# W ahead of the adjacency rows, the short row tile in the middle of its sums, and gathers of names and rows by turns, in a four-layer graph and expert network

## The chip, the cores and the metric

The kernel runs on one core of one Trainium2 chip, as one launch. The metric is the time of that launch on the device in microseconds (us), the median of several runs; less is better. The core's engines are TensorE (PE in the profile; its weight loads are PEld), VectorE (DVE), ScalarE (ACT), GpSimd (POOL) and SyncE (SP). In this kernel SP issues the large loads, and POOL issues the small loads and all indirect DMAs, the gathers and scatters by index.

## The reference

`x` is 2708 x 256, `adj` is 2708 x 2708, all float32. There are four layers, each of a graph step that adds a product with a matrix made from `adj`, and an expert or dense step. The change touches layers 0 and 1. `layernorm` is over the last axis. Cut to these two:

```python
# layer 0, graph step
msg = layernorm(x) @ W + B
weights = where(adj < 1.0, exp(-(1 / adj - 1) ** 2 / (2 * 0.5 * 0.5)), 0)
x = x + weights @ msg
# layer 0, experts: the best two of eight, softmax of their two scores
...
# layer 1, graph step
A = adj + eye(2708)
D = 1 / sqrt(sum(A, axis=1))
x = x + relu((A * D[:, None] * D[None, :]) @ (layernorm(x) @ W) + b)
# layer 1, experts: one hidden layer for all, then the best of eight second matrices
xf = layernorm(x)
H = gelu(xf @ W1 + b1)                 # 2708 x 1024
probs = softmax(H @ Wg + bg)
out = zeros_like(xf)
for e in range(8):
    y = H @ Wd[e] + bd[e]
    out = out + where(argmax(probs) == e, probs[:, e] * y, 0)
x = x + out
```

Layers 2 and 3 are two attention layers over the same neighbours, one with two experts for all rows and one with a dense step.

## The kernel before

**Tiles.** The 2708 rows make 22 row tiles of 128; the last one, number `FULL` = 21, has 20 rows (`LAST`). A graph step is done for a group of output tiles at a time, which hold their sums in PSUM: layer 0 has groups of 9, 7 and 6 tiles (`GROUPS`), layer 1 of 8, 8 and 6 (`GROUPS1`). For each group the loop over `j` goes over the row tiles of `adj`: a piece `adrow` of 128 rows and the group's columns is loaded by SP, made into weights, and multiplied into the group's sums. In layer 0 the weights need ACT and DVE (`y`, `wt`, L813 to L824), in layer 1 only the diagonal is added (L1096), and a mask of the positive entries is kept for the later layers (L1093). In layer 0 these products are at L863, in layer 1 at L1124.

**The last row tile.** Its 20 rows would use 20 of TensorE's 128 rows. `last_rows` (L278) fills a tile with ones by a memset on POOL and loads the 20 rows into its four quadrants with several small DMAs on SP (L282); `last_product` (L286) then multiplies from these quadrants. In layer 0 this happens inside the loop, in layer 1 it is the last pass of the loop, `j == FULL`, and its products end the sums (`stop`).

**The start.** Layer 0 begins with the products of `layernorm(x) @ W` as the first group's loop goes along: `W` is loaded by POOL through `mat` (L127), its column sums come from four matmuls (L796), DVE subtracts them (L798), and L241 multiplies a tile of transposed `x` with the result. `xT` and `x` are loaded by SP, two tiles at a time, between the rows of `adj` (L806, L56, L838).

**Layer 1's experts.** After each group, `send1` computes the hidden rows (L347 and on), writes them to the DRAM tensor `hid` (L1047), finds each row's expert, and scatters the row's number and score into `taken` at places sorted by expert (`route`, then L481). A unit of the expert step is 128 places of one expert, and class `Units` handles it: a gather of the 128 row numbers and scores (`fetch_names`, L495), a gather of those hidden rows, 512 KB, into one of three buffers (`fetch_rows`, L625), the expert's second matrix, 1152 KB, by SP into one of three buffers `wb` (`weights1`, L971), the transposition of the rows (L635, copied by ACT at L636), 16 matmuls (L674), bias and score on DVE (L675, L676), and a scatter to `given` (L481). Nine units (`NA`) can be known from the first two groups; `begin` prepares them within the third group's sums, and the first of them are run between the steps of the third group's `send1`. The other 15 wait for its scatters. `more` (L646) issues names and rows so that at most four units have names fetched and three have rows.

**Order.** The program's order on each engine is that of a scheduler, within the data dependences; `pin()` fixes what came before it, and manual edges with no wait (`NoSync`) can fix the order of two instructions on their engine. All indirect DMAs go through POOL one after the other; a DMA on POOL also waits for the one issued eight before it, and one on SP for an earlier one of its lane in the same way. The buffers `wb` lie where the sums' buffers were, so W2's first reads wait for the end of the third group's sums. The layers' small vectors and matrices come on POOL as well; layer 3's `w_l3` (L1210) is loaded there while layer 1's units run, and `score_columns` (L250, L251) multiplies it on DVE.

Of the kernel before, what the change touches and what calls it, by code (L numbers as in the profile page):

```python
# [8 lines left out]
F32 = mybir.dt.float32  # L9
# [6 lines left out]
P = 128  # L16
N = 2708
D = 256
DC = D // P
E = 8  # L20
NT = (N + P - 1) // P
W = 512
Q = P // 4

FULL, LAST = N // P, N % P
# [41 lines left out]
def adj_ffn4(ctx: ExitStack, tc: tile.TileContext, a: dict, out: bass.AP):  # L67
    nc = tc.nc
# [75 lines left out]

    pin()

    def rsqrt(pool, val, n):


        y = pool.tile([P, n], F32, name="rs_y", tag=f"rs_y{n}", bufs=2)  # L150
        q = pool.tile([P, n], F32, name="rs_q", tag=f"rs_q{n}", bufs=2)
        v.tensor_scalar(q.bitcast(I32), val.bitcast(I32), 1, None, op0=ALU.logical_shift_right)
        v.tensor_scalar(y.bitcast(I32), q.bitcast(I32), -1.0, float(0x5F3759DF), op0=ALU.mult,
                        op1=ALU.add)
        for _ in range(3):
            v.tensor_tensor(q, y, y, ALU.mult)
            v.scalar_tensor_tensor(q, q, -0.5, val, op0=ALU.mult, op1=ALU.mult)
            v.scalar_tensor_tensor(y, q, 1.5, y, op0=ALU.add, op1=ALU.mult)
        return y
# [115 lines left out]
                      stop=True, tile_position=(0, z))  # L275
        s.copy(values, p[:, :n])

    def last_rows(dst, parts):  # L278

        g.memset(dst, 1.0)  # L280
        for q, k, c0, w in parts:
            nc.sync.dma_start(dst[q * Q : q * Q + LAST, k : k + w],  # L282
                              a["adjT"][FULL * P :, c0 : c0 + w])
# [209 lines left out]
    def gather(dst, src, ix, bound, group, past):  # L493

        i = g.indirect_dma_start(out=dst, out_offset=None, in_=src,  # L495
                                 in_offset=bass.IndirectOffsetOnAxis(ap=ix, axis=0),
                                 bounds_check=bound, oob_is_err=False)
        tc.declare_no_dep(i.ins, group=group, keep=past, reason="rows of other groups")
        tc.add_to_no_dep_group(group + "read", i.ins)
        behind(i, past)  # L500


    XW = D + 2
# [96 lines left out]
    class Units(Blocks):  # L600
# [2 lines left out]

        def __init__(self, pool, given, weights, hidden):
            Blocks.__init__(self, pool, given, weights)
            self.hidden, self.named, self.places = hidden, [], [0, 0]

            self.names = pool.tile([P, MOST, 2], F32, name="names")
            g.memset(self.names, 1.0)
            self.hs = pool.tile([P, 3, HC * P], F32, name="hs")  # L610
            g.memset(self.hs, 0.0)
            self.ik, self.ok = "taken1", "given1"

        def fetch_names(self, item):
            (_, ix, _), b, past, src, full = item
            m = self.names[:, self.places[0], :]
            self.places[0] += 1
            gather(m, src, ix[:, b, :], src.shape[0] - 1, self.ik, past)
            self.named.append((m, src.shape[0]))

        def fetch_rows(self):
            m, n = self.named.pop(0)
            h = self.hs[:, self.places[1] % 3, :]
            self.places[1] += 1
            g.indirect_dma_start(out=h, out_offset=None, in_=self.hidden[:n, :],  # L625
                                 in_offset=bass.IndirectOffsetOnAxis(ap=m[:, 0:1].bitcast(I32), axis=0),
                                 bounds_check=n - 1, oob_is_err=False)
            self.rows.append((m, h))

        def turn(self, pool, h):  # L630
# [92 lines left out]
    with ExitStack() as l0:  # L723
# [17 lines left out]
        gate, gnn, sums = ExitStack(), ExitStack(), ExitStack()  # L741
        tp = gate.enter_context(tc.tile_pool(name="t0", reuse_waits="tile", bufs=2))
        gp = gnn.enter_context(tc.tile_pool(name="g0", reuse_waits="tile", bufs=3))
        w_sb = mat(gp, "L0_gnn_W", D)
        b_bc = row_bc(gp, "L0_gnn_B", D)
        wg = mat(tp, "L0_ffn_Wg", E)
        bg = row_bc(tp, "L0_ffn_bg", E)
# [78 lines left out]
        for tiles in GROUPS:  # L826
# [8 lines left out]
            for j in range(FULL):  # L835
                r = rows(j)
                ad = gp.tile([P, GMAX * P], F32, name="adrow", bufs=5)[:r, :w]
                i = nc.sync.dma_start(ad, a["adjT"][j * P : j * P + r, c0 : c0 + w])  # L838
                reads.append(i.ins.name)
                if begin and j % 2 == 0:  # L840
                    for t0 in (j,) if j < FULL - 3 else (j, j + 2) if j == FULL - 3 else ():
                        front(t0)
                if begin and j == FULL - 2:
                    spread_out(msg[:, FULL, :])
                if j == (FULL - 2 if begin else 12):
                    cols = [gp.tile([P, GMAX * P], F32, name=name, tag=name, bufs=bufs)[
                        :, : (1 + max(k for _, k in places.values())) * P]
                            for name, bufs in (("adrow", 5), ("y", 3), ("wt", 4))]
                    last_rows(cols[0], [(places[n][0], places[n][1] * P, c0 + n * P,
                                         min(2, len(own) - n) * P) for n in range(0, len(own), 2)])  # L850
                    weigh(*cols, P)
                    for n, t, _ in by_turns(own):
                        last_product(acc[n // 2][:, n % 2, :], places[n][0], cols[2],
                                     places[n][1] * P, msg[:, FULL, :], False)
                y = gp.tile([P, GMAX * P], F32, name="y", bufs=3)[:r, :w]
                wt = gp.tile([P, GMAX * P], F32, name="wt", bufs=4)[:r, :w]
                weigh(ad, y, wt, r)
                for p, pair in zip(acc, pairs):
                    for n in pair:
                        if n == len(own):  # L860
                            continue
                        _, k, q = own[n]
                        te.matmul(p[:q, n - pair[0], :], lhsT=wt[:, k : k + q],  # L863
                                  rhs=msg[:r, j, :], start=(j == 0 and n == pair[0]),
                                  stop=(j == FULL - 1 and n == pair[-1]))
                if end and j == 2:
                    cols = [gp.tile([P, GMAX * P], F32, name=name, tag=name, bufs=bufs)[
                        :, : NT * Q].rearrange("p (t c) -> p t c", c=Q)
                            for name, bufs in (("adrow", 5), ("y", 3), ("wt", 4))]
                    last_columns(cols[0])  # L870
                    weigh(*cols, P)
                    last = last_sums(acc[-1].rearrange("p k d -> p (k d)"), cols[2],
                                     lambda j, r: msg[:r, j, :], D)
                    v.tensor_tensor(x[:LAST, FULL, :], x[:LAST, FULL, :], last, ALU.add)
                if end and j == NT - 5:
                    past = list(scattered["taken0"])
                    items = [(full, b, past, taken[0][: 2 * held], True) for b in range(NA)]
                    for item in items[:2]:
                        work0.fetch_rows(item)
# [81 lines left out]
    with ExitStack() as l1:  # L961
# [2 lines left out]
        b1 = tp.tile([P, HC], F32, name="b1")  # L964
        g.dma_start(b1, a["L1_ffn_b1"])
        hw = l1.enter_context(tc.tile_pool(name="h1", side="right", reuse_waits="tile", bufs=1))
        wbs = {}

        def weights1(b, e):
            wb = wbs["pool"].tile([P, 2048 + D], F32, name="wb", bufs=3)  # L970
            nc.sync.dma_start(wb, a["L1_ffn_Wdp"][bass.ds(e, 1)].rearrange("e p n -> p (e n)"))  # L971
            return wb.rearrange("p (f d) -> p f d", d=D)

        gate, gnn, sums = ExitStack(), ExitStack(), ExitStack()
# [91 lines left out]
        for tiles in GROUPS1:  # L1066
# [11 lines left out]
                v.scalar_tensor_tensor(x[:q, t : t + m, :], o, 0.0, x[:q, t : t + m, :],  # L1078
                                       op0=ALU.max, op1=ALU.add)

            for j in range(NT):
                r = rows(j)
                if j == FULL:

# [2 lines left out]
                        spread_out(sup[:, FULL, :])  # L1087
                ad = gp.tile([P, 8 * P], F32, name="adrow", tag="adrow", bufs=4)[:r, :w]
                if j < FULL:
                    nc.sync.dma_start(ad, a["adjT"][j * P : j * P + r, c0 : c0 + w])  # L1090
                else:
                    last_rows(ad, [(q, 0, c0, w) for q in range(P // Q)])
                v.tensor_scalar(mask[:r, j, c0 : c0 + w], ad, 0.0, None, op0=ALU.is_gt)  # L1093
                for t, k, q in own:
                    if t == j:
# [18 lines left out]
                if j == FULL:  # L1114
                    for n, t, k in by_turns(own):
                        last_product(acc[n // 2][:, n % 2, :], n // 2, ad, k, sup[:, FULL, :],
                                     n == pairs[n // 2][-1])
                    continue
                for p, pair in zip(acc, pairs):
                    for n in pair:  # L1120
                        if n == len(own):
                            continue
                        _, k, q = own[n]
                        te.matmul(p[:q, n - pair[0], :], lhsT=ad[:, k : k + q],  # L1124
                                  rhs=sup[:r, j, :], start=(j == 0 and n == pair[0]), stop=False)
            for p, pair in zip(acc, pairs):
                if pair[0] < len(own):
                    t, m = own[pair[0]][0], len(pair)
# [602 lines left out]
```

## Time and profile before

| | |
|---|---|
| median of 3 runs | 2036.22 us (2031.78 to 2037.07) |
| the profiled execution, its span | 2048.93 us, 2047.2 us |
| mean granted TensorE clock | 0.967 of full speed |
| TensorE, from the page | 1916.4 us busy in 9641 instructions |
| DMA | 243.93 MB, mean 119 GB/s over the span |

The profiled execution is one run, recorded with its instructions; its times in the views are us from the start of its span. The whole span in 40 equal slices of 51 us, each digit a busy share in tenths (PEclk: the granted clock, GB/s: what the DMA engines moved):

```profile
PE   7999979999997999999796889999999999999997
DVE  7687842543434333344341165555445588987876
ACT  8777722222224203022221152223234400120112
POOL 1004362333321000102345300000000000000000
PEclk9999979999998999999897999999899999999998
DMA  8435567877744343534666720000101000000000
```

Layer 0's graph step fills slices 1 to 5, and its experts those up to about 632 us. Layer 1's sums run from there to 996 us, its third group from 881; the units and the third group's `send1` from 996 to 1168 (slices 20 to 23). Layers 2 and 3 follow. The queues that the change moves work between or reorders, with packets, MB and share of the 16 DMA engines' time (q1 is SP's, q0 is POOL's):

```profile
q1 hardware_dynamic: 69596, 196.81, 29.0%
q0 software_dynamic: 17232, 45.38, 6.5%
```

In the groups of waits, a line names the engine and the line that waited, what it waited for, and then the total in us, how many times, and the longest one. In the timeline, a line is start, length, engine, line, operation, output and inputs, count, and in brackets how long the engine had been idle before it and what ended that. By line a helper's number can stand for several tiles, so the tile's name is read with it.

### The profile page before, as it was taken

Reading aid. Unit: us, or ns where it says so; the run is one execution under the profiler, and the core shown is the slowest. Engines: PE = TensorE matmul, PEld = TensorE weight load, DVE = VectorE, ACT = ScalarE, POOL = GpSimd, SP = SyncE. Lnnn points to the kernel's source line nnn. Section 1 sums busy time; section 2 is a strip of 40 time slices with the busy share of each in tenths; the row PEclk is TensorE's granted clock in tenths of the full one; section 3 lists DMA queues with packets and bytes.
Section 4 is the critical chain, followed back from the end, with each engine's and each line's share of the span. In section 5 each row is a group of like instructions: output and inputs, shape, how many; then the busy total and the mean of one; then the engine's idle time right before and its main releaser. Section 6 shows DMA issues by size and latency. Waiting matters only on the chain.

```text
span 2047.2 us, 25961 instructions
## 1 busy us (share of the span) xinstructions
PE 1916.4 (94%) x9641; PEld 1374.6 (67%) x9641; DVE 1103.8 (54%) x2503; ACT 639.0 (31%) x1407; POOL 333.0 (16%) x369
## 2 busy tenths in 40 slices
PE   7999979999997999999796889999999999999997
PEld 5888868888886788878675768887576522232334
DVE  7687842543434333344341165555445588987876
ACT  8777722222224203022221152223234400120112
POOL 1004362333321000102345300000000000000000
PEclk9999979999998999999897999999899999999998
DMA  8435567877744343534666720000101000000000
GB/s 267 144 101 156 171 219 269 324 289 303 268 175 126 119 137 111 144 86 121 200 200 234 304 69 1 1 1 1 41 1 32 16 1 21 21 26 11 16 11 24
DMA packets 86960, 243.93 MB, mean 119 GB/s; under 512 B 17151, under 2 KB 40919, under 8 KB 77612
## 3 DMA queue, kind: packets, MB, share of 16 engines
q1 hardware_dynamic: 69596, 196.81, 29.0%
q0 software_dynamic: 17232, 45.38, 6.5%
q8 instruction: 79, 1.29, 0.3%
q14 instruction: 53, 0.43, 0.1%
HBM read 216.54 MB, written 28.97 MB: 120 GB/s over the span
## 4 chain that ended last, share of the span: by engine, by line
PE 55%; issue 5%; DMA 5%; DVE 4%; POOL 3%; ACT 2%; POOLq 0%; SPq 0%; DVEq 0%; ACTq 0%
PE num L1643 11%; PE ps_acc L1319 9%; PE acc L1124 8%; PE ps_tmp L347 7%; PE den L1654 6%; PE ps_acc L1495 3%; PE ps_tmp L241 3%; DMA given<-ys,xs 2%; PE ps_tmp L198 1%; PE ps_acc L241 1%; PE ps_tmp L1045 1%; POOL given L481 1%; POOL names L495 1%; PE yacc L674 1%; DMA adrow<-in_adjT 1%
## 5 line engine op out<-in xcount | busy, mean ns | idle before, releaser
L1638 DVE SCALAR_TENSOR_TENSOR e<-arena,G,mask 128x1024 f32<-128x1024 f32 (+2 forms) x264 | 294.2, 1150 | 41.1 <-PE den L1654 40.7
L1643 PE MATMUL num<-e,wh 128*64 128x512 f32 (+4 forms) x1056 | 240.9, 553 | 0.3 <-ACT L_gnn_W L1176 0.3
L1124 PE MATMUL acc<-sup,adrow 128*128 128x256 f32 x882 | 200.7, 385 | 2.8 <-DVE o L1076 1.5
L1319 PE MATMUL ps_acc<-hh,e 128*128 128x257 f32 x882 | 199.2, 382 | 2.0 <-ACT o L1264 2.0
L863 PE MATMUL acc<-msg,wt 128*128 128x256 f32 x882 | 198.1, 381 | 2.4 <-DVE x L886 1.2
L1124 PEld LDWEIGHTS acc<-sup,adrow 128*128 128x128 f32 x882 | 166.4, 192 | 31.0 <-issue 4.6
L578 PE MATMUL ps_acc<-xTs,wa 128*128 128x256 f32 x768 | 179.5, 387 | 6.1 <-issue 3.3
L863 PEld LDWEIGHTS acc<-msg,wt 128*128 128x128 f32 x882 | 165.2, 190 | 28.1 <-DVE wt L824 2.1
L1319 PEld LDWEIGHTS ps_acc<-hh,e 128*128 128x128 f32 x882 | 163.7, 190 | 29.6 <-ACT o L1264 5.0
L1643 PEld LDWEIGHTS num<-e,wh 128*64 128x64 f32 (+1 forms) x1056 | 73.9, 136 | 153.2 <-issue 119.9
L587 PE MATMUL yacc<-wb,hTs 128*128 128x256 f32 x768 | 175.5, 381 | 0.5 <-DVE ys L589 0.5
L580 ACT ACTIVATE hTs<-ps_acc,wa 128x256 f32<-128x256 f32 x192 | 90.8, 475 | 259.4 <-PE yacc L587 172.0
L578 PEld LDWEIGHTS ps_acc<-xTs,wa 128*128 128x128 f32 x768 | 142.1, 192 | 35.2 <-ACT hTs L580 5.3
L587 PEld LDWEIGHTS yacc<-wb,hTs 128*128 128x128 f32 x768 | 145.2, 191 | 20.3 <-DVE ys L589 0.9
L1654 PE MATMUL den<-e,wh 128*32 128x512 f32 (+4 forms) x1056 | 138.2, 553 | 0.0
L1313 DVE SCALAR_TENSOR_TENSOR e<-Rb,G,mask 128x640 f32<-128x640 f32 (+2 forms) x110 | 85.2, 775 | 92.8 <-PE ps_acc L1319 92.7
L199 ACT COPY xT<-ps_tmp 128x256 f32<-128x256 f32 x120 | 40.7, 364 | 276.5 <-PE ps_tmp L198 275.4
L1093 DVE TENSOR_SCALAR mask<-adrow 128x1024 uint8<-128x1024 f32 (+1 forms) x66 | 41.4, 630 | 134.5 <-DMA adrow<-in_adjT 134.5
L674 PE MATMUL yacc<-wb,hTs 128*128 128x256 f32 x384 | 94.7, 400 | 7.6 <-DVE ys L675 3.8
L589 DVE TENSOR_TENSOR ys<-yacc,wb 128x256 f32<-128x256 f32 x48 | 20.4, 424 | 134.3 <-PE yacc L587 134.3
L1654 PEld LDWEIGHTS den<-e,wh 128*32 128x32 f32 (+1 forms) x1056 | 30.9, 108 | 90.0 <-issue 86.7
L674 PEld LDWEIGHTS yacc<-wb,hTs 128*128 128x128 f32 x384 | 75.1, 202 | 19.2 <-DVE ys L675 4.1
(423 smaller groups left out, 2660.4 us busy)
## 6 DMA issues: line engine op xcount, KB each, us to landing
adhalf<-in_adjT SPq DMA_DIRECT2D x42, 677.0 KB
wb<-in_L_ffn_W2p SPq DMA_DIRECT2D x24, 1152.0 KB
wb<-in_L_ffn_Wdp SPq DMA_DIRECT2D x24, 1152.0 KB
wa<-in_L_ffn_W1b SPq DMA_DIRECT2D x24, 1028.0 KB
adrow<-in_adjT SPq DMA_DIRECT2D x42, 512.0 KB
adrow<-in_adjT SPq DMA_DIRECT2D x42, 320.0 KB
adrow<-in_adjT SPq DMA_DIRECT2D x21, 576.0 KB
hid<-hrow POOLq DMA_DIRECT2D x21, 512.0 KB
```

The source lines that it names most:

```text
L347: te.matmul(p[:, :w], lhsT=w1[:, c, f * P : (f + 1) * P], rhs=xnT[:, c, c0 : c0 + w], start=(c == 0), stop=(c == DC - 1))
L578: te.matmul(p[:, f % 2, :], lhsT=w1[:, c, f * P : (f + 1) * P], rhs=xT[:, c, :], start=(c == 0), stop=(c == DC - 1))
L580: s.activation(hT[:, f, :], p[:, f % 2, :], AF.Gelu, bias=bias[:, f : f + 1])
L587: te.matmul(q[:, k, :], lhsT=hT[:, f, k * P : (k + 1) * P], rhs=w2[:, f, :], start=(f == 0), stop=(f == HC - 1))
L674: te.matmul(q, lhsT=hT[:, f, :], rhs=w2[:, f, :], start=(f == 0), stop=(f == HC - 1))
L863: te.matmul(p[:q, n - pair[0], :], lhsT=wt[:, k : k + q], rhs=msg[:r, j, :], start=(j == 0 and n == pair[0]), stop=(j == FULL - 1 and n == ...
L1124: te.matmul(p[:q, n - pair[0], :], lhsT=ad[:, k : k + q], rhs=sup[:r, j, :], start=(j == 0 and n == pair[0]), stop=False)
L1313: v.scalar_tensor_tensor(e[:r, :w], Rb[:r, c0 : c0 + w], G[:r, j, :], mask[:r, j, c0 : c0 + w], op0=ALU.max, op1=ALU.mult)
L1319: te.matmul(p[:, : D + 1], lhsT=e[:, k : k + q], rhs=hh[:, j, :], start=(j == 0), stop=False)
L1638: v.scalar_tensor_tensor(e[:r, :w], Rb[:r, k, :w], G[:r, j, 2 * pair + k, :], mask[:r, j, c0 : c0 + w], op0=ALU.max, op1=ALU.mult)
L1643: te.matmul(num[k * DK : (k + 1) * DK, hf, :q], lhsT=wh[:r, j, 2 * pair + k, :DK], rhs=e[:r, h0 - c0 : h0 - c0 + q], start=(j == 0), stop= ...
L1654: te.matmul(den[z : z + Q, :q], lhsT=wh[:ri, i, 2 * pair + k, DK : DK + 1].to_broadcast([ri, Q]), rhs=e[:ri, h0 - c0 : h0 - c0 + q], start ...
```

## The change

Four edits in layers 0 and 1. No arithmetic is added or left out.

- Layer 0's `W` is loaded by SP, as its first read, and each read of `adj` is kept behind the one before it, the first behind `W`.
- In layer 1 the short row tile `FULL` is taken after row tile 11 and not after 20, in every group; row 20 now ends the sums. The fill with ones is done there by DVE (`v`) and not by POOL; in layer 0 it stays on POOL (`g`).
- Each read of `wb` in layer 1 is kept behind the last read of `adj` that the program issued before it.
- In `Units`, each gather of names is kept behind the last gather of rows that the program issued before it (`self.got`). `gather` returns its instruction for this.

`after` adds an edge of order with no wait.

```diff
+    def after(i, past):
+
+        tc.add_manual_dep(i.ins, past, mybir.DependencyInfo(
+            mybir.DependencyClass.NoSync, mybir.DependencyReason.DATA), reason="order")
...
-    def last_rows(dst, parts):
-
-        g.memset(dst, 1.0)
+    def last_rows(dst, parts, filler):
+
+        filler.memset(dst, 1.0)
...
         behind(i, past)
+        return i
...
-            self.hidden, self.named, self.places = hidden, [], [0, 0]
+            self.hidden, self.named, self.places, self.got = hidden, [], [0, 0], None
...
-            gather(m, src, ix[:, b, :], src.shape[0] - 1, self.ik, past)
+            i = gather(m, src, ix[:, b, :], src.shape[0] - 1, self.ik, past)
+            if self.got is not None:
+
+                after(i, self.got)
...
-            g.indirect_dma_start(out=h, out_offset=None, in_=self.hidden[:n, :],
+            i = g.indirect_dma_start(out=h, out_offset=None, in_=self.hidden[:n, :],
...
+            self.got = i.ins.name
...
-        w_sb = mat(gp, "L0_gnn_W", D)
+        w_sb = gp.tile([P, DC, D], F32, name="L0_gnn_W", bufs=1)
+        first = nc.sync.dma_start(w_sb, a["L0_gnn_W"].rearrange("(c p) n -> p c n", p=P))
...
                 i = nc.sync.dma_start(ad, a["adjT"][j * P : j * P + r, c0 : c0 + w])
+                after(i, reads[-1] if reads else first.ins.name)
                 reads.append(i.ins.name)
...
-        wbs = {}
+        wbs, reads = {}, []
...
-            nc.sync.dma_start(wb, a["L1_ffn_Wdp"][bass.ds(e, 1)].rearrange("e p n -> p (e n)"))
+            i = nc.sync.dma_start(wb, a["L1_ffn_Wdp"][bass.ds(e, 1)].rearrange("e p n -> p (e n)"))
+            after(i, reads[-1])
...
-            for j in range(NT):
+            for j in [*range(12), FULL, *range(12, FULL)]:
...
-                    nc.sync.dma_start(ad, a["adjT"][j * P : j * P + r, c0 : c0 + w])
+                    i = nc.sync.dma_start(ad, a["adjT"][j * P : j * P + r, c0 : c0 + w])
+                    reads.append(i.ins.name)
                 else:
-                    last_rows(ad, [(q, 0, c0, w) for q in range(P // Q)])
+                    last_rows(ad, [(q, 0, c0, w) for q in range(P // Q)], v)
...
-                                     n == pairs[n // 2][-1])
+                                     False)
...
-                                  rhs=sup[:r, j, :], start=(j == 0 and n == pair[0]), stop=False)
+                                  rhs=sup[:r, j, :], start=(j == 0 and n == pair[0]),
+                                  stop=(j == FULL - 1 and n == pair[-1]))
```

More of the change, by code (lines that the diff above doesn't have):

```diff
@@ L849, in adj_ffn4 @@
                     last_rows(cols[0], [(places[n][0], places[n][1] * P, c0 + n * P,
-                                         min(2, len(own) - n) * P) for n in range(0, len(own), 2)])
+                                         min(2, len(own) - n) * P) for n in range(0, len(own), 2)], g)
                     weigh(*cols, P)
```

## The prediction, written before the change was run

> **What bounds the kernel now.** I read the page's busy shares and chain first, then TensorE's own waits, then the busy time by stage, last the timeline where those waits lie.
>
> ```profile
> PE 1916.4 (94%) x9641; PEld 1374.6 (67%) x9641; DVE 1103.8 (54%) x2503; ACT 639.0 (31%) x1407; POOL 333.0 (16%) x369
> ...
> PE 55%; issue 5%; DMA 5%; DVE 4%; POOL 3%; ACT 2%; POOLq 0%; SPq 0%; DVEq 0%; ACTq 0%
> ```
>
> TensorE is busy 94% of the span, so a change that leaves its work alone can win only its waits and the stretches at a lower granted clock. The waits that the change can reach:
>
> ```profile
> PE ps_tmp L796 <- DMA L_gnn_W<-in_L_gnn_W: 9.2, 1, 9.2
> PE acc L286 <- DMA adrow<-in_adjT: 7.8, 1, 7.8
> PE ps_acc L635 <- DMA hs<-hid,names: 7.3, 2, 6.6
> PE ps_tmp L241 <- DVE L_gnn_W L798: 6.0, 1, 6.0
> PE ps_acc L635 <- ACT hTs L636: 5.1, 2, 3.2
> PE yacc L674 <- DVE ys L675: 3.8, 1, 3.8
> ```
>
> By stage (columns: length; busy us and count of PE, PEld, DVE, ACT, POOL; granted clock; DMA share; GB/s):
>
> ```profile
> 20.00:40.00 20.00, 20.00 (x89) 17.33 (x88) 18.45 (x36) 18.28 (x21) 0.00 (x0) 1.00 0.84 277
> 986.00:1007.00 21.00, 11.04 (x44) 8.63 (x45) 11.33 (x39) 2.95 (x6) 7.25 (x8) 0.67 0.65 214
> 1047.00:1116.00 69.00, 48.62 (x233) 41.01 (x233) 17.02 (x60) 9.77 (x18) 45.60 (x47) 0.85 0.71 220
> 1116.00:1160.00 44.00, 43.26 (x239) 38.28 (x238) 7.78 (x20) 10.74 (x20) 18.30 (x18) 1.00 1.00 399
> ```
>
> From 20 us on layer 0's sums fill TensorE, so time won ahead of them stays won. At 986 and from 1047 to 1116 TensorE has holes and a low clock; in the second POOL is busy 45.6 of 69 us with 47 instructions. From 1116 TensorE is full again, beside DMA at 1.00. The two holes:
>
> ```profile
> 989.89 1.00 POOL L495 DMA_INDIRECT names<-taken,b_ix  x1 [0.30 <-issue]
> 990.89 0.65 POOL L280 MEMSET adrow<- 128x640 f32 x1
> 991.56 1.42 SPq L282 DMA_DIRECT2D adrow<-in_adjT  x4
> 993.47 2.45 PE L286 MATMUL acc<-sup,adrow 20*128 20x256 f32 x10 [7.81 <-DMA adrow<-in_adjT]
> 995.84 3.17 PE L635 MATMUL ps_acc<-ident,hs 128*128 128x128 f32 x16
> 1001.31 4.08 PE L674 MATMUL yacc<-wb,hTs 128*128 128x256 f32 x10 [2.29 <-DMA wb<-in_L_ffn_Wdp]
> ```
>
> The sums are over at 985.65. The filler memset of the last row tile stands behind four gathers of names on POOL, the tile's loads behind the memset, and TensorE idles 7.81 us.
>
> ```profile
> 1072.27 0.99 POOL L625 DMA_INDIRECT hs<-hid,names  x1 [0.30 <-issue]
> 1078.80 1.03 POOL L625 DMA_INDIRECT hs<-hid,names  x1 [0.30 <-issue]
> 1080.55 1.94 PE L635 MATMUL ps_acc<-ident,hs 128*128 128x128 f32 x8 [6.57 <-DMA hs<-hid,names]
> 1097.94 0.77 POOL L1210 DMA_DIRECT2D w_l<-in_L_gnn_WT  x1
> 1110.23 2.22 PE L674 MATMUL yacc<-wb,hTs 128*128 128x256 f32 x6 [3.83 <-DVE ys L675]
> ```
>
> An indirect DMA holds POOL 1.0 us and 0.3 us more; three or four names between two gathers of rows put 6.5 to 8.5 us between rows, where a unit (16 matmuls L674, 3.47, and 8 of L635, 0.87) needs 4.33. The layer-3 matrix, last in POOL's queue, lands 9.8 us later (1107.74); DVE has waited 9.57 us for it at L250, ahead of the sum `ys`, and TensorE waits for DVE.
>
> **What the Trainium skill says.** "DMA: Bandwidth & Descriptors", Anatomy of one DMA: a POOL-issued DMA costs about 2.0 us plus bytes over 436 GB/s, and waits sit on the issuing sequencer, not in the DMA engines. Where the DMA engines are quiet (1090), names land 2.0 to 2.4 us after issue, which agrees; the 256 KB W takes 7.1, because (same page, Issuing engines are not separate DMA queues) all queues share 16 engines: its neighbours are six reads of SP's. "TensorE: Matmul & The Clock Gate", Part 1: an idle window of about 3.4 us halves the clock; the 0.67 at 986 agrees. "VectorE: DVE Perf Modes", Zero memsets can be issued as uint32: a memset takes a cycle per element whatever the type, so I scale below.
>
> **Part 1, layer 0.** W now goes first on SP; POOL loses one issue. All of SP's reads move one issue (0.4 us) and 256 KB back, about 0.8 us at the 313 GB/s of 0 to 20 us. W was issued at 1.91 and landed at 9.03; issued at 0.83 with nothing ahead it lands at about 5 (adrow 0 did, at 4.97). The pair of L798, which DVE ran at 16.74 behind statistics and weights, stands ahead of them in the new order. TensorE then can start L241 when xT of tile 2 is there (it landed at 14.6, plus 0.8: 15.4); three tiles of L241 stand before row 0. Before, row 0's sums began at 21.63; now at about 16 to 18. Row 1's weights come at 21.9 at best, since ACT has one layer-norm waiting for adrow 3 (about 18.5) ahead of them. So by 21.9 one row (18 records, 3.97) and one tile of L241 (0.93) more are done: 4.9, taken as 5. Bounds: 1 (row 0 itself waits for ACT) to 8 (row 1 isn't late either).
>
> **Part 2, layer 1's last row tile.** FULL goes between rows 11 and 12 in three groups; its memset moves from POOL (1.51 or 0.65 us) to DVE: 128x128 took 0.17 us, so 1024 columns some 1.1 to 1.4 us by the page's rule. DVE is busy 18.7 of 39 us in the last group, which hides it; in the middle group it stands ahead of one diagonal sum that TensorE needs: up to 1.5 us, 0.5 taken. Its four SP loads are tiny, but in the last group they fall among the taken scatters, where reads land 5.7 to 7.6 us after issue; TensorE idled 0.96 there at 966.6 and may idle 3. So the sums end at 985.65 plus 10 matmuls at full clock (16 took 1.15, so 0.7) plus 2 more idle, less 0.8 where it overlaps: 987.5, against 995.92: 8.4. Behind it work runs at a higher clock: L635 x16 at 2.1 and not 3.17, L674 x10 at 2.3 and not 4.08. W2's reads still can't start before the sums' buffers are free (0.1 us after their end; landing 5.1 later), so the idle of 2.29 stays. 8.4 + 2.8 less 0.5 = 10.7; bounds 5 (idle of 7 in the middle) to 13. Order edges of W2's reads behind adj's only fix what the queue does now: nothing.
>
> **Part 3, names and rows by turns.** The number of indirect DMAs is the same. In POOL's new order a unit is given, rows, names: 3 x 1.31 = 3.93, under 4.33. By hand, with the route some 10 us earlier (about 1037), the six scatters issued 1040 to 1048 and landed near 1053, first names 1055, rows of unit 10 at 1060.6, landed 1066.5. DVE now waits for the layer-3 matrix before the seventh `ys` (issued about 1058.6, landed by 1068), so the weights' slot for unit 10 frees late: its L674 at 1075, with about 6 + 4 us of idle around it. Before, it started at 1087.31; units 10, 11, 12 then took 28.3 us to 1115.6 instead of 13.0. So 12.3 + 15.3 = 27.6 ahead, of which 10.7 is part 2's: 16.9. Against it: (a) the short halts at 1091 to 1098 (3 x 1.13 "issue", 3.17 for ACT), which have no cause on POOL: half of 6.6 kept, 3.3; (b) names now stand in the saturated stretch. Rows k+2 need names issued five instructions earlier, 2c - 1.31 us, c the time of a unit. Names follow a rows gather in the same queue, and rows landed +9.5 there, so names would land at +8.4, asking c = 4.85. But fewer rows would be in flight then, and names are small (their packets take 0.01 us): I take 4.4, between 4.33 and 4.85: 15 x 0.07 = 1. Part 3: 12.6; bounds 3 and 18.
>
> **Sum.** 5 + 10.7 + 12.6 = 28.3. The profiled execution took 2048.93 (span 2047.2), so about 2020.6; it stands 12.7 above the median 2036.22 of the runs shown, which gives 2007.9. I forecast 2008. Layers 2 and 3 (1180 to 2047) aren't touched.
>
> **Rivals.**
> A, the units give it back: names late in the queue (c = 4.85 costs 15 x 0.52 = 7.8), all halts stay (3.3 more). For it: DMA is at 1.00 from 1116, so no earlier start shortens that. Against: the window 1047 to 1116 moves only 220 GB/s. Gain 28.3 - 10.1 = 18: 2018.
> B, layer 0's start isn't kept: ACT (18.28 of 20) and DVE (18.45) are nearly as full as TensorE at 20 to 40, and row 1 onward may pace by them. Gain 23: 2013, inside the forecast's range.
> C, slower: the turn serialises. Rows wait on POOL for names, and everything behind (given, next names) waits with them. It loses when 15(c - 4.33) exceeds 28.3 + 1, c = 6.3, which needs names to land 2c - 1.31 = 11.3 us after issue; at c = 6.9 it is 10 slower: 2046. For it: taken scatters at +10.0, rows at +9.8. Against: names never over 7.1.
> D, it doesn't do what it says: W shares the engines with adrow and lands as late, the last row's idle just moves, c is near 5: 2034.
>
> **How the numbers follow.** About 0.3% (6 us) is what a measurement can tell from no change. Forecast (2001 to 2016, B in it) 0.56; A (2016 to 2026) 0.23; below 2001 0.04; D 0.07; C 0.10. Faster 0.83, same 0.07, slower 0.10. The range 1999 to 2029 leaves out C and most of D.
>
> **What would show it.** Step 1: first L863 before 18. Step 2: no wait at L286 over 4, sums over before 989. Step 3: rows at most 5.5 us apart on POOL, unit 10 before 1078, units at 4.3 to 4.5. It is wrong if TensorE waits for `hs` in every unit, or if the DVE stall on the layer-3 matrix reaches TensorE for more than 6.

## The result and the profile after

| | before | after |
|---|---|---|
| median, us (4 runs each) | 2036.64 (2031.78 to 2040.77) | 2012.41 (2009.97 to 2015.35) |
| profiled execution, its span, us | 2048.93, 2047.2 | 2009.97, 2008.2 |

The ratio is 0.9883, with a 95% interval of 0.9857 to 0.9908: 24 us less, between 19 and 29. The forecast was 2008, which is 28 us less.

The two profiles are 39 us apart, more than the medians. Layer 0's experts, which nothing in the change touches, took 349.8 us from first to last matmul at L578 (L584 after) in the profile of before and 342.9 in that of after. The experiments below show that this belongs to the session and not to the kernel. So from here on stages are compared, within one session where there is a pair.

The page's line of TensorE and the waits of TensorE in the profile after (columns: who waited for whom; us in total, times, longest). Lines have moved: L246 was L241, L291 was L286, L645 was L635, L684 was L674, L807 was L796.

```profile
PE 1902.1 (95%) x9641; PEld 1364.3 (68%) x9641; DVE 1106.0 (55%) x2506; ACT 636.7 (32%) x1407; POOL 329.5 (16%) x365
```

```profile
PE ps_acc L645 <- DMA hs<-hid,names: 10.9, 7, 5.4
...
PE ps_tmp L246 <- DMA xT<-in_xT: 6.2, 1, 6.2
...
PE yacc L684 <- DMA wb<-in_L_ffn_Wdp: 3.9, 4, 2.6
PE ps_tmp L807 <- DMA L_gnn_W<-in_L_gnn_W: 3.9, 1, 3.9
...
PE acc L291 <- DMA adrow<-in_adjT: 2.8, 1, 2.8
```

Every wait of the prediction's list has got shorter or gone, but one: the wait for `W` is 3.9 and not 9.2, VectorE's step on it (L798, 6.0) is at 0.5, the one at the last row tile 2.8 and not 7.8, those for `ys` and for `hTs` don't appear. The wait for rows has grown from 7.3 in two places to 10.9 in seven. At the start the wait for `W` has a successor, 6.2 us for `xT`.

The start of layer 0 on TensorE (timeline):

```profile
3.86 2.05 PE L807 MATMUL ps_tmp<-L_gnn_W,all_ones 128*128 128x256 f32 x4 [3.86 <-DMA L_gnn_W<-in_L_gnn_W]
6.42 3.78 PE L246 MATMUL ps_tmp<-L_gnn_W,xT 128*128 128x256 f32 x8 [0.52 <-DVE L_gnn_W L809]
16.42 3.78 PE L246 MATMUL ps_tmp<-L_gnn_W,xT 128*128 128x256 f32 x8 [6.22 <-DMA xT<-in_xT]
19.99 4.29 PE L875 MATMUL acc<-msg,wt 128*128 128x256 f32 x18
```

`W` is there 5.3 us sooner, but the sums start only 1.6 sooner (19.99 against 21.63): behind the first two tiles of `x`, two more stand ahead of row 0 in TensorE's order. Their `xT` comes at 16.4, and their 8 matmuls run at a granted clock of 0.50 (16 to 20 us).

The end of layer 1's third group (timeline):

```profile
951.24 1.66 PE L291 MATMUL acc<-sup,adrow 20*128 20x256 f32 x10 [2.84 <-DMA adrow<-in_adjT]
952.83 21.37 PE L1138 MATMUL acc<-sup,adrow 128*128 128x256 f32 x90
974.04 2.91 PE L645 MATMUL ps_acc<-ident,hs 128*128 128x128 f32 x24
979.58 5.38 PE L684 MATMUL yacc<-wb,hTs 128*128 128x256 f32 x16 [2.63 <-DMA wb<-in_L_ffn_Wdp]
```

The last row tile stands in the middle, with 2.84 us of idle. Behind the sums the wait for the first W2 is still there, and the 16 matmuls after it take 5.38 us, where 16 of them at full clock take 3.62: the granted clock over them is 0.68.

The stages (columns: length; busy us and count of PE, PEld, DVE, ACT, POOL; granted clock; DMA share; GB/s), the second one from unit 10 on:

```profile
1026.00:1062.00 36.00, 29.03 (x154) 25.20 (x155) 13.69 (x53) 6.05 (x12) 26.35 (x29) 0.91 0.83 264
1062.00:1106.00 44.00, 40.21 (x217) 34.33 (x216) 7.60 (x20) 9.39 (x18) 27.44 (x28) 1.00 0.95 351
```

Before, the full stretch of units had TensorE busy 43.26 of 44 us beside DMA at 1.00. Now this stretch begins 88 us after the sums and not 120, but has TensorE at 40.21 and DMA at 0.95: something else holds it. POOL's timeline shows what:

```profile
1077.26 1.00 POOL L500 DMA_INDIRECT names<-taken,b_ix  x1 [0.31 <-issue]
1078.56 1.02 POOL L486 DMA_INDIRECT given<-ys,names  x1 [0.30 <-issue]
1079.89 1.02 POOL L634 DMA_INDIRECT hs<-hid,names  x1 [0.30 <-PE yacc L684]
1081.22 1.00 POOL L500 DMA_INDIRECT names<-taken,b_ix  x1 [0.31 <-issue]
1083.45 1.01 POOL L486 DMA_INDIRECT given<-ys,names  x1 [1.23 <-DVE ys L686]
1086.82 1.01 POOL L634 DMA_INDIRECT hs<-hid,names  x1 [2.36 <-PE ps_acc L645]
```

The gather of rows at 1086.82 uses the names issued five instructions earlier, at 1077.26. The profile puts its 2.36 us down to a TensorE turn, but the buffer's own turn (of the rows issued three gathers earlier) had been over since 1080.5. By the trace's semaphore updates those names landed at 1086.08, 8.8 us after their issue and 0.74 before the rows' start. The same for the last gathers in a row:

```
rows issued   their names issued   landed            from landing to issue
1086.82       1077.26              1086.08 (+8.8)    0.74
1090.76       1081.22              1089.97 (+8.8)    0.79
1095.82       1088.14              1095.07 (+6.9)    0.75
1101.40       1092.09              1100.66 (+8.6)    0.74
1105.76       1097.14              1105.02 (+7.9)    0.74
1110.18       1102.73              1109.44 (+6.7)    0.74
```

The names in turn landed 0.2 to 0.7 us after the 512 KB of rows that had been issued just before them (for the six: 1085.91, 1089.24, 1094.90, 1100.07, 1104.84 and 1109.09). So here the names set the pace. From unit 10 to the last, a unit takes 4.78 us (1061.62 to 1128.61, 14 steps); in 11 of these 15 units the rows start within 1 us of their names' landing, in the other four 2.3 to 4.7 us after it.

### The profile page after: what moved, and what is told of

Its sections match the earlier page's. It is cut to its first block, busy times and chain, and to the rows that moved or that the text cites. A ratio compares the mean times of both kernels' runs of the same rounds, so it can differ in the third digit from the quotient of the medians.

```text
span 2008.2 us, 25964 instructions
## 1 busy us (share of the span) xinstructions
PE 1902.1 (95%) x9641; PEld 1364.3 (68%) x9641; DVE 1106.0 (55%) x2506; ACT 636.7 (32%) x1407; POOL 329.5 (16%) x365
## 5 line engine op out<-in xcount | busy, mean ns | idle before, releaser
L584 PE MATMUL ps_acc<-xTs,wa 128*128 128x256 f32 x768 | 177.1, 384 | 2.0 <-DVE xTs L557 1.9
L593 PE MATMUL yacc<-wb,hTs 128*128 128x256 f32 x768 | 174.1, 379 | 0.5 <-DVE ys L595 0.5
L584 PEld LDWEIGHTS ps_acc<-xTs,wa 128*128 128x128 f32 x768 | 141.2, 191 | 30.4 <-DVE xTs L557 5.3
L593 PEld LDWEIGHTS yacc<-wb,hTs 128*128 128x128 f32 x768 | 144.1, 190 | 19.6 <-DVE ys L595 1.1
L684 PE MATMUL yacc<-wb,hTs 128*128 128x256 f32 x384 | 91.8, 390 | 3.9 <-DMA wb<-in_L_ffn_Wdp 3.9
L835 DVE SCALAR_TENSOR_TENSOR wt<-adrow,wt 128x640 f32<-128x640 f32 (+3 forms) x67 | 71.0, 1061 | 27.2 <-ACT wt L141 26.6
```

What stands on the lines that cost most here:

```text
L584: te.matmul(p[:, f % 2, :], lhsT=w1[:, c, f * P : (f + 1) * P], rhs=xT[:, c, :], start=(c == 0), stop=(c == DC - 1))
L593: te.matmul(q[:, k, :], lhsT=hT[:, f, k * P : (k + 1) * P], rhs=w2[:, f, :], start=(f == 0), stop=(f == HC - 1))
L684: te.matmul(q, lhsT=hT[:, f, :], rhs=w2[:, f, :], start=(f == 0), stop=(f == HC - 1))
```

## The experiments

Each kernel was timed in turns with before on the same chip. There were three sessions, each on another chip, on which before's own median was 2048.15, 2038.88 and 2048.05 us; so across sessions the ratios are the safer comparison. "us" is the ratio's difference from 1 times before's 2036.64. The stages come from one profile of each: layer 1's sums (start of the first matmul to start of the last), and the rest (from there to the start of the last unit's last matmul).

| kernel | ratio, 95% interval | us | layer 1's sums | the rest |
|---|---|---|---|---|
| session 1: before again | - | - | 322.2 | 172.2 |
| W first | 0.9982 (0.9968 to 0.9996) | -3.7 | 322.8 | 174.4 |
| row in the middle | 0.9945 (0.9924 to 0.9966) | -11.2 | 312.1 | 166.8 |
| turns | 0.9936 (0.9916 to 0.9957) | -13.0 | 318.7 | 162.0 |
| session 2: the whole change | 0.9877 (0.9857 to 0.9898) | -25.1 | 311.5 | 158.8 |
| five names ahead | 0.9893 (0.9871 to 0.9916) | -21.8 | 311.7 | 155.5 |
| layer 3's matrix late | 0.9906 (0.9888 to 0.9923) | -19.1 | 310.4 | 168.6 |
| fill on VectorE alone | 0.9970 (0.9957 to 0.9982) | -6.1 | 315.7 | 177.1 |
| session 3: middle, fill on POOL | 1.0009 (0.9994 to 1.0024) | +1.8 | 327.7 | 166.9 |
| without the turns | 0.9909 (0.9880 to 0.9937) | -18.5 | 310.2 | 167.8 |
| five ahead for the rest | 0.9862 (0.9837 to 0.9887) | -28.1 | 311.0 | 158.9 |

**The parts one by one.** Before plus the edits of one part:

```diff
# W first
-        w_sb = mat(gp, "L0_gnn_W", D)
+        first = nc.sync.dma_start(w_sb, a["L0_gnn_W"].rearrange("(c p) n -> p c n", p=P))
...
+                after(i, reads[-1] if reads else first.ins.name)
# row in the middle
-            for j in range(NT):
+            for j in [*range(12), FULL, *range(12, FULL)]:
...
+                    last_rows(ad, [(q, 0, c0, w) for q in range(P // Q)], v)
# turns
+                after(i, self.got)
```

> Part 1 alone: W first on SP and adj's reads kept in order, nothing else changed. The theory (the time won before the first sums is kept, since TensorE is full behind them): the trace of the whole change has the first sums 1.6 us and the last sums of layer 0 3.5 us earlier, so 3 to 5 us less than before, ratio 0.998, and the rest of the kernel as before (idle of about 8 us at the last row tile, gaps at hs). Rival B (layer 0's sums pace by ScalarE and VectorE and give it back): 0 to 1 us.

> Part 2 alone: the short row tile between rows 11 and 12, its fill on VectorE, order of W2's reads. The theory: the idle of 7.8 us before the last products goes, about 3 us of idle come in the middle, and some of the slow clock behind it goes; 8 to 11 us less than before, ratio about 0.995. Rival (the units are bound by POOL's order of names and rows anyway and give it back): 0 to 3 us less.

> Part 3 alone: names behind rows on POOL; the fill stays on POOL but now has one gather of names ahead of it and not four, and layer 3's matrix comes after 6 and not 8 scatters of units. The theory: the units gain 9 to 13 us, and the idle before the last products shrinks by about 3.9 us; 11 to 16 us less, ratio about 0.993. A unit takes about 4.7 us where names wait behind rows, against 4.33 before. Rival A: the units' gain is eaten by the names, 3 to 6 us less in all.

The row in the middle also holds the order of W2's reads, which was not run apart. In the two kernels below without it, W2's first read still goes out within 0.2 us of the end of the sums, so it seems to change nothing.

All three are faster, W first only just. W first ends layer 0's sums at 256.7 and not 259.1 (before again), which is kept. The row in the middle takes 10.1 us out of layer 1's sums. Its rest is 5.4 us shorter as well, for which nothing in it gives a reason. W first, which touches nothing there, has it 2.2 longer, so a difference of a few us in the rest of two single profiles says little. The turns take 10.2 out of the rest, and 3.5 out of the sums, because now one gather of names and not four stands before the fill:

```profile
995.44 1.54 PE L291 MATMUL acc<-sup,adrow 20*128 20x256 f32 x10 [3.93 <-DMA adrow<-in_adjT]
```

The three add up to 27.9; the whole is 25.1 (session 2) and, in the runs with the result, 23.8. The intervals allow for that, and an overlap of 3.5 would be just this piece, which parts 2 and 3 both win.

**Before once more.**

> The kernel before once more, for a second profile. The profiled execution of before lies 12.7 us above its median. If that is one disturbed execution, this profile has a span of about 2034, layer 0's experts take some 343 us from first to last and not 349.8, and the halts of 1.1 us in the ninth to tenth unit are gone. If it belongs to the kernel, all three are as before.

One execution, 2050.69. Layer 0's experts take 351.1, and the halts are still there, so the first profile was no mishap. But it isn't the kernel either. In session 1 all four profiles have experts of 349.3 to 351.1 us; in session 2 all four, the kernel with nothing but the fill changed among them, 342.0 to 343.4; in session 3 350.5 to 351.0. The halts go with it. In the profile of before again, TensorE and ScalarE in the unit after the names in fours:

```profile
1098.77 0.57 PE L635 MATMUL ps_acc<-ident,hs 128*128 128x128 f32 x2 [1.83 <-issue]
1102.32 1.11 PE L635 MATMUL ps_acc<-ident,hs 128*128 128x128 f32 x4 [2.99 <-ACT hTs L636]
1101.68 1.56 ACT L636 COPY hTs<-ps_acc 128x512 f32<-128x512 f32 x3 [15.20 <-remote]
```

ScalarE stands still there for 15.2 us, put down to "remote", which is what the view prints where it doesn't know the releaser. Such a halt (ScalarE "remote" in the units) is in all profiles of sessions 1 and 3, with turns (1.5 and 5.4 us) and without (8.2 to 24.6 in sum), and in none of session 2, nor in the profile after. The profiles with halts, the first of before among them, also hold fewer records of DMA landings, about 8,460 to 8,610 against 10,130 in the others. Session and chip changed together, so what halts the engines, and which of the two it hangs on, stays open.

**The whole change again, with one name more ahead, and with layer 3's matrix late.**

```diff
# five names ahead
-            while self.names_todo and len(self.named) + len(self.rows) < 4:
+            while self.names_todo and len(self.named) + len(self.rows) < 5:
# layer 3's matrix late
-        g.dma_start(wa[:, :, :D], a["L3_gnn_WT"].rearrange("(c p) n -> p c n", p=P))
+        late = g.dma_start(wa[:, :, :D], a["L3_gnn_WT"].rearrange("(c p) n -> p c n", p=P))
+        after(late, scattered["given1"][8].name)
```

> The whole change once more, on one chip with the three that follow. The parts alone gave ratios 0.9982, 0.9945 and 0.9936, which add up to 0.9863, if each keeps what it won: 28 us. Rival: the parts overlap (the turns alone already shorten the idle at the last row tile), ratio 0.988 to 0.990. Layer 0's experts take 350 us in the profile, as in the kernels with one part, if the 342.9 of the first profile of this kernel was that execution's; 343 again if the change makes it.

> The whole change with names fetched for five units and not four, so that a gather of rows follows its names by eight instructions on POOL and not five. Theory: in the trace of the change each gather of rows starts 0.7 to 0.8 us after its names land, so names set the pace of 4.7 us a unit; with one more ahead the pace falls to the 4.33 to 4.4 of TensorE and DMA, 4 to 6 us less than the whole change. Rival: the DMA engines set it (share 1.00 before): within 1 us of the whole change.

> The whole change, but layer 3's matrix kept behind the ninth scatter of a unit on POOL, near where it was before. Theory of a second cause: part of what the turns won is that this matrix now lands before the units run at full pace, so VectorE's wait for it no longer stands before TensorE; then this is 3 to 8 us slower than the whole change, with a wait of VectorE for w_l and of TensorE for ys in the units. Rival: only the spacing of rows matters, then the same within 1 us.

With five names ahead, from unit 12 on a gather of rows starts 2.7 us or more after its names have landed, and doesn't wait for them. The unit falls from 4.80 to 4.55 us (units 10 to 24). The same stretch of both kernels, the whole change first:

```profile
1077.00:1129.00 52.00, 47.54 (x255) 40.71 (x253) 7.79 (x20) 12.42 (x22) 26.64 (x27) 1.00 0.95 349
```

```profile
1077.00:1129.00 52.00, 50.66 (x280) 44.32 (x279) 9.30 (x24) 13.43 (x25) 28.54 (x29) 1.00 0.99 387
```

TensorE goes from 47.5 to 50.7 busy of 52, DMA from 0.95 to 0.99. So names were the limit, and the DMA engines are likely the next one just behind it. The rest of layer 1 is 3.3 us shorter, but the whole time isn't: it came out 3.3 us longer than the whole change, within the intervals, and the 4 to 6 us expected are not seen. In its profile layer 1's sums begin 4.5 us later, behind stages that this edit doesn't touch.

Layer 3's matrix late costs 5.9 us by the two ratios, whose intervals just overlap, and 9.8 us of the rest in the trace. VectorE and TensorE in its profile:

```profile
1081.60 0.76 DVE L255 TENSOR_TENSOR o<-w_l,L_gnn_a_r 128x256 f32<-128x256 f32 x2 [9.84 <-DMA w_l<-in_L_gnn_WT]
```

```profile
1080.69 1.06 PE L645 MATMUL ps_acc<-ident,hs 128*128 128x128 f32 x8 [0.92 <-DMA hs<-hid,names]
1084.72 1.50 PE L684 MATMUL yacc<-wb,hTs 128*128 128x256 f32 x4 [2.96 <-DVE ys L685]
```

It is before's picture: VectorE waits 9.84 us for the matrix, ahead of a `ys`, and TensorE waits for VectorE. Some 5 of the 9.8 us stand at these two units. Another 5 stand near the end, behind a wait of 3.33 us for rows at 1130.66, which isn't the matrix's. In the whole change (the profile after) VectorE waits too, but TensorE is waiting for rows anyway:

```profile
1051.46 0.76 DVE L255 TENSOR_TENSOR o<-w_l,L_gnn_a_r 128x256 f32<-128x256 f32 x2 [7.30 <-DMA w_l<-in_L_gnn_WT]
1054.53 1.94 PE L645 MATMUL ps_acc<-ident,hs 128*128 128x128 f32 x8 [5.37 <-DMA hs<-hid,names]
```

So part of what the turns won isn't the spacing of rows; it is that fewer gathers of names stand before that matrix in POOL's queue (11 in the whole change, all 24 in before). How much is left for the spacing, the times don't show: the whole change with the matrix late (19.1 us less than before) can't be told from the whole change without the turns (18.5, below). The traces of session 2 show where it goes. From the start of unit 10's products to that of unit 14's it took 33.1 us with names in fours (the fill on VectorE alone, below), 23.8 with turns and the matrix late, and 18.6 in the whole change. From there to unit 24's it took 47.2, 51.4 and 48.6. What the turns win in the first stretch they give back in part in the second. A kernel with the matrix early and names in fours would settle the split; none was run.

**The place and the filler of the row tile.**

```diff
# fill on VectorE alone: the tile stays last
+                    last_rows(ad, [(q, 0, c0, w) for q in range(P // Q)], v)
# middle, fill on POOL
+            for j in [*range(12), FULL, *range(12, FULL)]:
```

> Before, with the fill of layer 1's last row tile on VectorE and nothing else; the tile stays the last pass. Theory: the idle of 7.8 us comes from the fill's place behind gathers on POOL; VectorE fills once row 17 is multiplied, the loads land before the sums need them, and 7 to 10 us go, about all that part 2 won. Rival: the tile has to leave the last place, since its loads then land late anyway: 0 to 3 us.

> Before, with the short row tile between rows 11 and 12 and nothing else: the fill stays on POOL, where in the third group it stands behind eight scatters. Theory (what matters is the queue that the fill stands in): the idle only moves into the middle of the third group, some 5 to 8 us at L286, since the scatters go out until about 968 while TensorE is at row 11 near 961; 0 to 4 us less than before. Rival (the place alone does it): as part 2 alone, 9 to 12 us less.

With the fill on VectorE and the tile last, the idle before L286 is gone and the sums are 6.5 us shorter than in before again, of another session. But much of it appears again at the next wait:

```profile
985.31 1.13 PE L286 MATMUL acc<-sup,adrow 20*128 20x256 f32 x10
986.37 1.09 PE L635 MATMUL ps_acc<-ident,hs 128*128 128x128 f32 x8
...
995.51 4.61 PE L674 MATMUL yacc<-wb,hTs 128*128 128x256 f32 x10 [6.82 <-DVE rs_y L158]
```

The releaser named, a step of VectorE, isn't it: W2's first read, issued at 986.61, landed at 995.37. It took 8.8 us where it took 5.1 before, most likely since now three gathers of rows, issued from 980.65 to 983.25, are still landing beside it (until 988.8): from 986 to 988 POOL's queue moved 0.57 MB and SP's 0.01. Before, they had landed within the idle (by 990.0). Of this wait 2.29 us were there before, so 4.5 are new. By the ratios the filler alone wins 6.1 of part 2's 11.2 us, less than the 7 to 10 expected. In the row-in-the-middle kernel these gathers go out 5 us sooner before the end of the sums, at 975.58 to 978.17, W2's read again takes 5.1, and the wait is 2.63. With the tile in the middle and the fill on POOL nothing is won:

```profile
979.92 2.04 PE L286 MATMUL acc<-sup,adrow 20*128 20x256 f32 x4 [10.39 <-DMA adrow<-in_adjT]
```

The fill now stands behind eight scatters, and the idle is larger, 10.39 us (5 to 8 expected), in the middle. So neither edit does it alone: the place alone wins nothing that can be measured, the filler alone about half.

**Without the turns, and five names ahead for the rest alone.** The whole change less part 3; and the whole change with

```diff
-            while self.names_todo and len(self.named) + len(self.rows) < 4:
+            while self.names_todo and len(self.named) + len(self.rows) < (4 if self.places[0] < 12 else 5):
```

> The whole change without part 3: W first and the short row tile in the middle, names on POOL as before. If the parts add up, 0.9982 x 0.9945 = 0.9927, some 15 us less than before, and the whole change is 10 us (0.9877 to 0.9883) better than this, all of it after the first unit that needs the third group's scatters. If part 3 overlaps with part 2, the whole is only 5 to 8 us better.

> The whole change, with names fetched for five units and not four only from the thirteenth unit's names on, so that the first rows of the rest aren't delayed. With five from the start the units ran at 4.49 us and not 4.73 in the trace, but the first of them began 0.9 us later behind one more gather, and layer 3's matrix landed at 1064.9 and not near 1051. Expected: the pace of 4.4 to 4.5 from the eleventh unit to the last, the start as in the whole change; last unit 3 to 4 us earlier within the layer, ratio 0.986 to 0.987. Rival: with rows and W2 both at DMA's limit nothing is won, ratio 0.988 as the whole change.

Without the turns the ratio is 0.9909; its interval holds 0.9927, the product of parts 1 and 2, so this doesn't tell an overlap from none. Five ahead for the rest alone ran its units at 4.62 us (4.57 from unit 11 on, where 4.4 to 4.5 was expected), with an idle of 3.80 us at unit 10 that the profile puts down to nothing (perhaps a halt of the session). Its ratio, 0.9862, is the lowest of all; it can't be told from the whole change's 0.9877, so that no version is shown to beat it.

## Why the prediction was right, and where its sizes were off

**The direction and the sum** were right: 28.3 forecast, 24 measured. Each of the three parts wins when it is run alone; for parts 1 and 2 the waits that were named are the ones that went, for part 3 that holds in part only. By the traces of before again and the whole change again: layer 0's sums end 2.8 sooner, layer 1 from its first sum to the third group's hidden rows (L352) takes 323.8 and not 334.0, and from there to the last unit 146.5 and not 160.3. These are 2.8, 10.2 and 13.9, against 5, 10.7 and 12.6. The two profiles are of different sessions, so the last one holds the halts too.

**Part 1, 5 us.** It won 3.7 alone (0.8 to 6.5), 2.3 to 3.5 in the traces. The term that was too large is the start of row 0, "at about 16 to 18". `W` landed at 3.7, sooner than the 5 assumed, but `xT` of the next two tiles at 16.4 and not 15.4. Their 8 matmuls stand ahead of row 0 and took 3.8 us at the granted clock of 0.50, where the prediction has 0.93 for a tile. That gives 19.99; the mark of 18 was missed. That ScalarE and VectorE would give it back (rival B) isn't seen: over the seven profiles with W first and the six without, the sums start 2.2 us sooner in the mean and end 2.5 sooner. In one of the seven (five names ahead) nothing is left at the end.

**Part 2, 10.7 us.** Right in the sum, 11.2 alone, but its two pieces were not as told. The sums themselves won 10.1 and not 7.9: the other two groups' ends lost their small waits too (for `o` 1.5, at L286 0.6, for `xn` from 4.0 to 1.9). The 2.8 for the work behind the sums at a higher clock didn't come: from the last sum to L352 it was 11.8 us before again and 12.3 after again. Its first half is there, 24 transposes (L645) in 2.91 us at full clock, where 16 took 3.17 before. The second isn't: the wait for W2 is still 2.63, and from 979.62 to 983.03 TensorE was granted half its clock, so that the 16 matmuls behind the wait take 5.38. An idle of 2.63 us was enough for that here, less than the 3.4 that the prediction went by. The fill took 0.91 us for 1024 columns on VectorE, under the estimate of 1.1 to 1.4, and the 0.5 for the diagonal in the middle group doesn't appear.

**Part 3, 12.6 us.** Unit 10 was put 87.5 us after the sums (987.5 to 1075); it came 87.4 (after) and 87.9 (after again) behind their end. From there on, 15 units at 4.4 were to take 66; they took 70.7. The step that was mis-sized is (b), the names in the saturated stretch. Its formula, 2c - 1.31 for the time that names have, is what the trace shows, and so is the +8.4 (6.7 to 8.8 measured). The choice of 4.4 near the lower bound, on the ground that less in flight would land sooner, was wrong: the pace was 4.8, near the upper bound of 4.85. This is rival A's mechanism at nearly its full price, 14 x 0.4 = 5.6 us. With it 12.6 becomes 7.0; by the ratios the whole change is 6.5 us ahead of the one without the turns (give or take 7, from their intervals). Step (a), half of the halts kept, can't be judged, since they come and go with the session. The wait for layer 3's matrix went as told, ahead of the seventh `ys` and not before TensorE. But the prediction didn't price what it costs where it was; it stands unnamed in the 28.3 us of units 10 to 12. By the ratios 5.9 of the 13.0 us that the turns won alone hang on it, and 3.5 more are the fill's, which the prediction has under part 2. The 3.6 left for the spacing can't be told from nothing by these intervals. So it is in part luck that 12.6 lies so near 13.0.

**Rival C** needed names to land 11.3 us after issue; the worst from unit 10 on was 8.8. (Names issued at 982.56 took 10.4, but their rows went out 20.7 us later.) **Rival D** had the last row's idle just move. That is what happens, wholly or in part, with either half of part 2 alone, and not with both.

**The other marks.** The wait at L286 (2.84, under 4), the end of the sums and unit 10 were met. Two of step 3's were missed: rows stood up to 6.9 us apart on POOL and not 5.5 at most, and units took 4.8 and not 4.3 to 4.5. Of its two signs of being wrong neither came: TensorE waited for rows seven times in 24 units, and the wait for layer 3's matrix didn't reach it.

## What to carry to other kernels

A wait that is taken away is only won if what ends next comes sooner too. The fill on VectorE removed 7.8 us of idle and met a 6.8 us wait for a read that was now issued while gathers were landing; move the work that feeds the next step as well, and look at that wait in the new trace. Where a small gather and a large one take turns in one queue, count how many instructions lie between the small one and its user: here five gave 4.8 us a unit, and eight 4.55. An edit of order moves everything in its queue: before the gain is put down to what the edit was meant for, put the other things that moved (here one matrix) back where they were, and run that. A releaser that had long been done is a sign to look for a DMA's landing.

## What the runs showed of the hardware

A gather of names moves packets of 64 bytes or less. Where the DMA engines are quiet (share of 0.2 or less from issue to landing), those with all their 16 landing records landed after 2.4 to 2.9 us. (The 2.0 to 2.4 in the prediction were read from DMAs of which before's profile holds two to four of the 16.) Behind 512 KB gathers of rows in the same queue it was up to 8.8 us from unit 10 on, and up to 10.8 just behind the end of layer 1's sums (9.7 and 11.5 with five ahead). The same untouched stage, layer 0's experts, took 342 to 343 us in one session and 349 to 351 in two others, and ScalarE stood still for up to 17.6 us at a time in the latter. So a profile of one session, or chip, isn't to be set beside one of another without a stage that neither kernel changes.
